# A fused cross-attention and mixture-of-experts kernel: first loads in another order, two elementwise steps on other engines

## The chip, the cores and the metric

The kernel runs on one core of one Trainium2 chip. Its work is shared by TensorE (matrix products and transposes), VectorE, ScalarE and GpSimd (elementwise work and reductions) and the DMA engines; SyncE (SP) only issues transfers. Each engine works through its own queue in order and waits, at the head of that queue, for what the instruction there needs. The metric is the device time of one execution in microseconds (us).

## The reference, cut to what matters

`x` has 4 batches of 512 rows with 512 features; `ctx` has 4 batches of 1601 rows. All is float32.

```python
x = x + xattn(layernorm(x), ctx)          # 16 heads of 32 features
x = x + moe(layernorm(x))                 # 32 experts, 4 per row, and a shared part

def xattn(x, ctx):
    img, txt = ctx[:, :257], ctx[:, 257:]
    q = rms_norm(x @ q_w.T + q_b) * norm_q_w
    k, k_img = rms_norm(...) of txt and img, each with weights of its own
    v, v_img = txt @ v_w.T + v_b, img @ v_img_w.T + v_img_b
    return (softmax(q k / sqrt(32)) v + softmax(q k_img / sqrt(32)) v_img) @ o_w.T + o_b
```

The experts: a router picks 4 of 32 per row, each expert takes at most 80 rows; its two products, SiLU and a third product follow, weighted and added into the output.

## The kernel before, in words

The order of the instructions is written out by hand; each engine's queue follows the order of the calls in the source.

**Opening.** `ones`, `ident_b`, `pick`, `late`, `sums` and `parts` are small constants, filled on VectorE (`ones` on GpSimd) in L140 to L169. Then the loads are issued, all on SP's queue: two tiles of x (`load_x`, 128 rows each), the query weights `q_w`, the columns `q_b` and `norm_q_w` (`column`, L171: 512 numbers laid out as 128 partitions by 4), two more tiles of x, `k_w`, and so on (L195 to L204). A bias column is read with a step, so that it consists of 512 pieces of 4 bytes. VectorE then scales `norm_q_w` (L207) and adds the two value biases (L209, `v_b`).

**Queries.** `queries` (L484) makes for each of a batch's four tiles of x a triple from `turned_x` (L270): *measure* (mean and variance on VectorE, L219 and L221, then 1/sqrt on GpSimd in two instructions, L213 and L214), *norm* (subtract the mean and scale, L227, VectorE) and *turn* (four transposes on TensorE, L285, and a copy on ScalarE, L286). `feature_chunk` (L234) follows: products with the weights (L238), a square with bias on ScalarE (L242) and bias and weight on VectorE (L243). For the first batch the triples run one after another (L503). For each later batch they are done during the attention of the batch before it, in the loop described next.

**Attention.** Per batch, the keys of four blocks of context are made first (`keys`, stages named (block, chunk) in `side`). Then come four groups c = 0 to 3 of four heads each, with 13 tiles t of 128 keys. A step t does on TensorE: the scores from which VectorE takes the row maxima of the *next* group (`wave`, L328, maxima L342 and L344), the weighted sums of tile t-2 (`weighted`, L387), this tile's scores again, shifted by the maxima (L376 and L379), whose exponentials ScalarE takes (L380); and some filling work, the values of the next group (L298) or, at c = 3, the next batch's queries. GpSimd adds up the exponentials (`added`, L395, two instructions of 128x1024 per step); at c = 3 VectorE does that. At the end of a group `split` cuts the maxima in three bfloat16 parts (L349 to L359), which TensorE turns (L365). Matmul results go round eight PSUM banks, less those that hold the running outputs.

`later` is a list of due work: `later.after(n, f)` runs f at the n-th following call of `later.step()`, of which there is one per step t, per key chunk and, after the last batch, per unit of the shared part. `normalize` (L421) uses it: the denominators of a group go through DRAM, VectorE inverts them (L429), SP fetches the result spread over the partitions (`rb`, four transfers, L433), GpSimd multiplies the two outputs (text and image, tiles `po_s` in SBUF) by it (L436, L437), and one step later VectorE adds both and the value bias (L438) into `aoT`, which the output product reads.

At c = 2 the next batch's x is prepared: tile i is loaded at t = 3i, measured at 3i+1, normalized at 3i+2 and turned at 3i+3 (L662 and L671 to L680).

**Rest.** `residual` (L446) projects the attention's output, adds x and the bias `o_b`, takes the second layer norm (with the same `moments` and `centred`) and the router's logits. After the last batch the shared part runs in `units`, with the routing beside it on VectorE, then the 32 experts, whose weights are streamed in.

Of the kernel before, what the change touches and what calls it, by code (L numbers as in the profile page):

```python
# [9 lines left out]
F32 = mybir.dt.float32  # L10
BF16 = mybir.dt.bfloat16
# [7 lines left out]
P = 128  # L19
# [59 lines left out]
        body(tc, a, ident, mhalf, logits, x1_d, xw_d, xnT_d, den_d, rec_d, out)  # L79


class Later:


# [19 lines left out]
def body(ctx, tc, a, ident, mhalf, logits, x1_d, xw_d, xnT_d, den_d, rec_d, out):  # L104
# [31 lines left out]
    def held(name):  # L136
        return hold.tile([P, D], F32, name=name, tag="hold")


    ones = w.tile([P, P], F32, name="ones")  # L140
    nc.gpsimd.memset(ones, 1.0)
    ident_b = w.tile([P, P], BF16, name="ident_b")
    nc.vector.tensor_copy(ident_b, ident)

    pick = w.tile([P, 3, P], BF16, name="pick")
    nc.vector.memset(pick, 0.0)
    for r in range(0, P, HD):
        nc.vector.memset(pick[r:r + 3, 0, :], 1.0)
        nc.vector.memset(pick[r:r + 6, 1:3, :], 1.0)
        nc.vector.memset(pick[r:r + 3, 2, :], 0.0)  # L150
        nc.vector.memset(pick[r:r + 3, 1, HALF:], 0.0)

    late = w.tile([P, HALF], BF16, name="late")
    nc.vector.memset(late, 0.0)
    for r in range(0, P, HD):
        nc.vector.memset(late[r:r + 3, :], 1.0)
        nc.vector.tensor_copy(pick[r:r + 6, 1, :HALF], late[r:r + 6, :])

    sums = w.tile([P, 3, 2, HD // 2], F32, name="sums")
    nc.vector.memset(sums, 0.0)  # L160
    nc.vector.memset(sums[:, 0, 0, :], 1.0)
    nc.vector.memset(sums[:HALF, 1, 0, :], 1.0)
    nc.vector.memset(sums[HALF:, 1, 1, :], 1.0)
    nc.vector.memset(sums[:, 2, 1, :], 1.0)
    parts = []
    for n in range(2):
        t = w.tile([P, NQ, P], BF16, name=f"parts{n}", tag=f"parts{n}")
        nc.vector.memset(t, 0.0)
        parts.append(t)  # L169

    def column(name, src=None):  # L171
        t = w.tile([P, NC], F32, name=name, tag=name)
        nc.sync.dma_start(t, a[name] if src is None else src)
        return t

    def bias_column(name):
        return column(name, a[name].rearrange("(c p) -> p c", p=P))

    def weight(name, tile_=None, tag=None):
        t = w.tile([P, NC, D], F32, name=name, tag=tag or name) if tile_ is None else tile_  # L180
        nc.sync.dma_start(t, a[name])
        return t

    def load_x(b, qt):
        xt = rowt("xt")
        nc.sync.dma_start(xt, a["x"][b, qt * P:(qt + 1) * P, :])
        return xt
# [4 lines left out]
        nc.sync.dma_start(cT, a["ctxT"][b, :, s0:s0 + n].rearrange("(c p) t -> p c t", p=P))  # L192
        return cT

    first_x = [load_x(0, qt) for qt in range(2)]  # L195
    wq = weight("q_w")
    q_b, nq_w = bias_column("q_b"), column("norm_q_w")
    first_x += [load_x(0, qt) for qt in range(2, NQ)]
    first_wk = weight("k_w", wide("wk"))
    k_b, nk_w = bias_column("k_b"), column("norm_k_w")  # L200
    first_block = load_block(0, 0)
    wv = weight("v_w")
    ki_b, nki_w = bias_column("k_img_b"), column("norm_k_img_w")
    v_b, vi_b = bias_column("v_b"), bias_column("v_img_b")  # L204
    o_b = w.tile([P, D], F32, name="o_b")
    rw = w.tile([P, NC, E], F32, name="rw")
    nc.vector.tensor_scalar(nq_w, nq_w, SM_SCALE, None, ALU.mult)  # L207

    nc.vector.tensor_tensor(v_b, v_b, vi_b, ALU.add)  # L209

    def inv_sqrt(r, v, scale, eps):
        n = r.shape[1]
# [3 lines left out]
    def moments(src):  # L216

        stats = st.tile([P, 6], F32, name="stats")
        nc.vector.bn_stats(stats, src)  # L219
        mv = st.tile([P, 2], F32, name="mv")  # L220
        nc.vector.bn_aggr(mv, stats)  # L221
        r = st.tile([P, 1], F32, name="rstd")
        inv_sqrt(r, mv[:, 1:2], 1.0, 1e-5)
        return mv[:, 0:1], r

    def centred(dst, src, moments):
        nc.vector.tensor_scalar(dst, src, *moments, ALU.subtract, ALU.mult)  # L227

    def project(ps, lhsT, rhs):

# [39 lines left out]
    def turned_x(xlT, qt, xt):  # L270

        got = []

        def measure():
            got.append(moments(xt()))

        def norm():
            xl = rowt("xl")
            centred(xl, xt(), got.pop())
            got.append(xl)  # L280

        def turn():
            ps = psum()
            for c in range(NC):
                nc.tensor.transpose(ps[:, c * P:(c + 1) * P], got[0][:, c * P:(c + 1) * P], ident)  # L285
            nc.scalar.copy(xlT[:, :, qt * P:(qt + 1) * P], ps.rearrange("p (c t) -> p c t", c=NC))  # L286

        return measure, norm, turn
# [132 lines left out]
    def normalize(i, c, aoT, po_t, po_i, den):  # L421

        nc.sync.dma_start(den_d[i], den[0:P:HD // 2, :])
        dn = st.tile([P, 2 * NG4 * L // P], F32, name="dn")
        nc.sync.dma_start(dn, den_d[i].rearrange("r (k q) -> (r k) q", k=P // (2 * NG4)))

        def invert():
            rc = st.tile([P, 2 * NG4 * L // P], F32, name="rc")
            nc.vector.reciprocal(rc, dn)  # L429
            nc.sync.dma_start(rec_d[i].rearrange("r (k q) -> (r k) q", k=P // (2 * NG4)), rc)  # L430
            rb = mid.tile([P, 2, L], F32, name="rb")
            for g in range(NG4):
                nc.sync.dma_start(rb[g * HD:(g + 1) * HD], rec_d[i, 2 * g:2 * g + 2, :].partition_broadcast(HD))  # L433

            def scale():
                nc.gpsimd.tensor_tensor(po_t, po_t, rb[:, 0, :], ALU.mult)  # L436
                nc.gpsimd.tensor_tensor(po_i, po_i, rb[:, 1, :], ALU.mult)  # L437
                later.after(1, lambda: nc.vector.scalar_tensor_tensor(  # L438
                    aoT[:, c, :], po_t, v_b[:, c:c + 1], po_i, ALU.add, ALU.add
                ))  # L440

            later.after(2, scale)

        later.after(2, invert)
# [55 lines left out]
        return [partial(value_tile, v, c, t, cTs, ws) for t in range(NKT)]  # L500

    qT, sq_q, turn, work = queries(0, first_x, L)
    for f in [f for parts in turn for f in parts] + work:  # L503
        f()
    pending = []
    for b in range(B):
        kT = kv.tile([P, NC, S], F32, name="kT")
# [4 lines left out]
        rest = [[]] * NQ  # L512
        if b == 0:
            wvi = weight("v_img_w")
            nc.sync.dma_start(o_b, a["o_b"].partition_broadcast(P))
            nc.sync.dma_start(rw, a["router_w"])
        else:
            wo = weight("o_w", wide("wo"))
            rest = [residual(b - 1, qt, aoT, lambda wo=wo: wo) for qt in range(NQ)]
# [81 lines left out]
        for c in range(NC):  # L601
# [30 lines left out]
            for t in range(NKT):  # L632
                pT = wide("pT")
                pTs.append(pT)
                if more:
                    wave(c + 1, t, qT, kT, mx)
                if t == 0 and c:
                    mT = shifts(part, nc.scalar.copy)
                if t in (0, 2) and pending:
                    pending.pop(0)()  # L640
                if t == 1:
                    if more:
                        v_next = kv.tile([P, NKT, P], F32, name="v", bufs=2)
                        fill = values(v_next, c + 1, cTs, ws)
                        fill[0]()
                        done = 1
                    elif b + 1 < B:
                        fill = work
                if t > 1:
                    consume(t - 2)  # L650
                exps(c, t, qT, kT, mT, pT)
                if t == 0 and pending:
                    pending.pop(0)()
                if t == 2:
                    g["acc"] = begun(pTs, not more)
                elif 2 < t <= MIX:
                    added(g["acc"], pTs[t - 1], slice(0, P), not more)
                elif t == NKT - 1 and not more:
                    added(g["acc"], pTs[MIX], slice(0, HALF), True)
                if c == 0 and t < 3:  # L660
                    rest[t]()
                if c == NC - 2 and b + 1 < B and t and t % 3 == 0:  # L662
                    turn[t // 3 - 1][2]()
                while t and done * (NKT - 1) < len(fill) * t:
                    fill[done]()
                    done += 1
                later.step()
                if more and t == NKT - 1:
                    part = parts[(c + 1) % 2]
                    split(mx, part, NM)  # L670
                if c == NC - 2 and b + 1 < B:  # L671
                    if t == 0:
                        xs = []
                        qT_next, sq_next, turn, work = queries(b + 1, xs, P)
                    if t % 3 == 0 and t < 3 * NQ:
                        xs.append(load_x(b + 1, t // 3))
                    if t % 3 == 1 and t < 3 * NQ:
                        turn[t // 3][0]()
                    if t % 3 == 2:
                        turn[t // 3][1]()  # L680

            def image(consume=consume, pTs=pTs, idle=not more):

# [356 lines left out]
```

## Time and profile before

| | |
|---|---|
| time, median of 3 runs | 1780.51 us (1779.47 to 1783.83) |
| profiled execution, its own time | 1803.62 us |
| its span, first to last instruction | 1801.9 us |
| mean granted TensorE clock in it | 0.984 |
| TensorE (PE) busy | 1709.7 us, 95% |
| VectorE (DVE) busy | 1002.6 us, 56% |
| GpSimd (POOL) busy | 830.4 us, 46% |
| ScalarE (ACT) busy | 621.7 us, 35% |
| first TensorE instruction | 22.52 us |

In the timeline a line is: start, duration, engine, line of the source, operation, output<-inputs, sizes, and in brackets how long the engine had been idle and what ended that. A line with "x4" merges four instructions in a row. In the view of waits the three figures are the sum in us, how often, and the longest. In the windows each engine has its busy time and, in brackets, the instructions that began; the last three figures are the granted TensorE clock, the DMA share and GB/s. SPq and the like are an engine's queue issuing a transfer.

### The profile page before, as it was taken

The page shows a single profiled execution, that of the slowest core. Times are in us where ns is not written, and L with a number is a line of the kernel's source. Part 1 is how long each engine was busy: PE and PEld are TensorE (multiplying, and loading weights), DVE is VectorE, ACT ScalarE, POOL GpSimd, SP SyncE. Part 2 cuts the span into 40 slices and gives each one's busy share as a digit, 9 for nine tenths or more (in the row PEclk, how much of TensorE's full clock was granted, in tenths as well). Part 3 has the DMA queues.
Part 4 walks back from the last instruction along what each step waited for, and adds up shares of the span by engine and source line. Part 5 has one row for each costly group of instructions (what it writes and reads, how often), then busy time and mean ns, then how long its engine had stood idle before and what let it go on. Part 6 is the DMA issues. An engine that isn't in the chain of part 4 may idle for free. (4 is left out here: it accounts for less than half of the span.)

```text
span 1801.9 us, 29352 instructions
## 1 busy us (share of the span) xinstructions
PE 1709.7 (95%) x11825; PEld 899.0 (50%) x11825; DVE 1002.6 (56%) x1893; ACT 621.7 (35%) x1336; POOL 830.4 (46%) x564
## 2 busy tenths in 40 slices
PE   4999999999999999999999999998999999999886
PEld 2564444445644444565444445643442454477664
DVE  2485666658556657675566558556556668511110
ACT  1114444631254555114554631254456110011111
POOL 1319759322379662327679422377681100123332
PEclk9999999999999999999999999999999999999998
DMA  6000000040100003120001040300011363389894
GB/s 220 1 1 1 20 1 31 15 156 30 65 1 20 31 2 119 50 77 18 20 1 32 14 156 13 105 1 14 2 59 60 114 207 105 100 263 283 272 287 103
DMA packets 68023, 138.38 MB, mean 77 GB/s; under 512 B 16048, under 2 KB 28464, under 8 KB 65584
## 3 DMA queue, kind: packets, MB, share of 16 engines
q1 hardware_dynamic: 62768, 125.70, 20.7%
q0 software_dynamic: 5120, 10.82, 2.9%
q8 instruction: 93, 1.52, 0.3%
q14 instruction: 42, 0.34, 0.1%
HBM read 113.68 MB, written 22.81 MB: 76 GB/s over the span
## 5 line engine op out<-in xcount | busy, mean ns | idle before, releaser
L380 ACT ACTIVATE pT<-ps 128x512 f32<-128x512 f32 (+1 forms) x832 | 429.7, 603 | 385.7 <-PE ps L379 377.4
L342 DVE TENSOR_REDUCE mx<-ps 128x1 f32<-128x512 f32 (+1 forms) x576 | 330.5, 615 | 255.8 <-PE ps L328 255.8
L395 POOL TENSOR_TENSOR acc<-acc,pT 128x1024 f32<-128x1024 f32 x192 | 449.5, 2377 | 14.4 <-ACT pT L380 13.8
L298 PEld LDWEIGHTS ps<-v_w,cT 128*128 128x128 f32 (+1 forms) x1408 | 170.5, 188 | 103.2 <-DVE mx L342 55.3
L387 PE MATMUL po<-pT,v 128*32 128x512 f32 (+2 forms) x1792 | 221.9, 603 | 0.0
L379 PE MATMUL ps<-qT,kT 32*128 32x512 f32 (+1 forms) x1664 | 218.0, 594 | 0.0
L328 PE MATMUL ps<-kT,qT 32*128 32x512 f32 (+1 forms) x1536 | 205.1, 550 | 0.0
L298 PE MATMUL ps<-v_w,cT 128*128 128x128 f32 (+1 forms) x1408 | 199.0, 286 | 0.0
L238 PE MATMUL ps<-cT,wk 128*128 128x512 f32 (+1 forms) x384 | 153.9, 546 | 0.0
L316 DVE TENSOR_REDUCE mx<-ps 128x1 f32<-128x512 f32 (+2 forms) x256 | 128.2, 564 | 7.3 <-PE ps L313 7.2
L914 POOL DMA_INDIRECT out<-y,tok x32 | 45.4, 1420 | 146.4 <-DMA out<-y,tok 72.3
L376 PE MATMUL ps<-mT,pick 32*128 32x512 bf16 (+1 forms) x832 | 86.7, 386 | 23.0 <-DVE mx L342 19.6
L395 POOL TENSOR_TENSOR pT<-pT 65x1024 f32<-65x1024 f32 x24 | 56.0, 2352 | 109.1 <-PE po L387 89.4
L245 POOL TENSOR_TENSOR sq_k<-sq_k,sq 128x512 f32<-128x512 f32 (+2 forms) x48 | 49.6, 1033 | 122.6 <-ACT sq L242 122.6
L376 PEld LDWEIGHTS <-pick 32*128 32x128 bf16 (+1 forms) x832 | 21.8, 91 | 167.4 <-issue 164.1
L238 PEld LDWEIGHTS ps<-cT,wk 128*128 128x128 f32 x384 | 69.6, 190 | 70.5 <-issue 54.3
L904 DVE TENSOR_TENSOR ehT<-ehT,ps 128x160 f32<-128x160 f32 x32 | 10.3, 321 | 164.1 <-ACT ehT L903 164.1
L306 ACT COPY v<-ps 128x128 f32<-128x128 f32 (+1 forms) x208 | 59.7, 287 | 117.4 <-PE ps L298 116.8
L328 PEld LDWEIGHTS ps<-kT,qT 32*128 32x128 f32 x1536 | 80.4, 184 | 31.1 <-issue 10.4
L379 PEld LDWEIGHTS ps<-qT,kT 32*128 32x128 f32 (+1 forms) x1664 | 81.5, 181 | 27.4 <-issue 23.1
L387 PEld LDWEIGHTS po<-pT,v 128*32 128x32 f32 (+2 forms) x1792 | 34.6, 107 | 119.1 <-issue 109.8
L402 POOL TENSOR_TENSOR acc<-pT 128x1024 f32<-128x1024 f32 x24 | 56.7, 2386 | 79.8 <-ACT pT L380 55.3
(176 smaller groups left out, 2187.6 us busy)
## 6 DMA issues: line engine op xcount, KB each, us to landing
W_gate<-in_W_gate SPq DMA_DIRECT2D x32, 512.0 KB, 5.7
W_up<-in_W_up SPq DMA_DIRECT2D x32, 512.0 KB, 6.7
W_down<-in_W_down SPq DMA_DIRECT2D x32, 512.0 KB, 5.5
xt<-in_x SPq DMA_DIRECT2D x32, 256.0 KB, 2.8
cT<-in_ctxT SPq DMA_DIRECT2D x8, 1024.0 KB, 8.4
rb<-rec_d SPq DMA_DIRECT2D x64, 128.0 KB, 2.7
wk<-in_k_w SPq DMA_DIRECT2D x4, 1024.0 KB
wki<-in_k_img_w SPq DMA_DIRECT2D x4, 1024.0 KB, 10.2
```

Of the source, the lines that this page charges most:

```text
L238: nc.tensor.matmul(ps[:, :n], lhsT=wt[:, k, c * P:(c + 1) * P], rhs=xT[:, k, to], start=k == 0, stop=k == NC - 1)
L298: nc.tensor.matmul(ps[lo:hi, :], lhsT=cTs[bl][:, k, at:at + hi - lo], rhs=ws[bl == NB - 1][:, k, c * P:(c + 1) * P], start=k == 0, stop=k ...
L306: nc.scalar.copy(v[:n, t, :], ps[:n])
L316: nc.vector.tensor_reduce(mx[:, qt, g, bl:bl + 1], ps[:, :n], AX.X, ALU.max, negate=True)
L328: nc.tensor.matmul(ps[:, j * n:(j + 1) * n], lhsT=qT[r:r + HD, c, q * P:(q + 1) * P], rhs=kT[r:r + HD, c, k0:k0 + n], start=True, stop=True,)
L342: nc.vector.tensor_reduce(mx[:, qt, g, i:i + 1], ps[:, :m], AX.X, ALU.max, negate=True)
L376: nc.tensor.matmul(ps[:n], lhsT=pick[r:r + HD, kind(t), :n], rhs=mT[r:r + HD, :], start=True, stop=False)
L379: nc.tensor.matmul(ps[:n], lhsT=kT[r:r + HD, c, t * P:t * P + n], rhs=qT[r:r + HD, c, :], start=False, stop=True)
L380: nc.scalar.activation(pT[:n, g, :], ps[:n], AF.Exp)
L387: nc.tensor.matmul(po[r:r + HD, :], lhsT=v[rows, t, r:r + HD], rhs=pT[rows, g, :], start=start, stop=stop)
L395: (nc.vector if idle else nc.gpsimd).tensor_tensor(to[rows, h, :], to[rows, h, :], pT[rows, h, :], ALU.add)
L402: (nc.vector if idle else nc.gpsimd).tensor_tensor(acc[:, h, :], pTs[0][:, h, :], pTs[1][:, h, :], ALU.add)
```

## The change

- All four tiles of x are loaded first, then `q_w` in four pieces; `k_w`, the context and the other weights follow on SP as before. The columns and `o_b` are issued on ScalarE's queue.
- The constants and the addition of the value biases come after the first batch's query projection, the scaling of `norm_q_w` after its norms. For the first batch all four tiles are measured first.
- `moments` also gives `off` = -mean * rstd (one GpSimd instruction more, for the output's norm too), and the norm of the queries is a ScalarE activation, scale * x + off. `centred` (VectorE) stays for the output's norm.
- In `normalize`, GpSimd adds the two outputs, and two steps after the scaling ScalarE adds the bias.
- At c = 2 the next batch's steps have tables for their places: loads at t = 0, 1, 5, 7, measures at 2, 4, 7, 9, norms at 4, 6, 9, 11, turns at 5, 7, 10, 12.

```diff
+LOAD, MEASURE, NORM, TURN = (0, 1, 5, 7), (2, 4, 7, 9), (4, 6, 9, 11), (5, 7, 10, 12)
...
-    ones = w.tile([P, P], F32, name="ones")
...
     def column(name, src=None):
         t = w.tile([P, NC], F32, name=name, tag=name)
-        nc.sync.dma_start(t, a[name] if src is None else src)
+        nc.scalar.dma_start(t, a[name] if src is None else src)
...
-    first_x = [load_x(0, qt) for qt in range(2)]
-    wq = weight("q_w")
+    first_x = [load_x(0, qt) for qt in range(NQ)]
+    wq = w.tile([P, NC, D], F32, name="q_w")
+    for k in range(NC):
+        nc.sync.dma_start(wq[:, k, :], a["q_w"][:, k, :])
     q_b, nq_w = bias_column("q_b"), column("norm_q_w")
-    first_x += [load_x(0, qt) for qt in range(2, NQ)]
+    k_b, nk_w = bias_column("k_b"), column("norm_k_w")
     first_wk = weight("k_w", wide("wk"))
-    k_b, nk_w = bias_column("k_b"), column("norm_k_w")
     first_block = load_block(0, 0)
     wv = weight("v_w")
     ki_b, nki_w = bias_column("k_img_b"), column("norm_k_img_w")
     v_b, vi_b = bias_column("v_b"), bias_column("v_img_b")
     o_b = w.tile([P, D], F32, name="o_b")
+    nc.scalar.dma_start(o_b, a["o_b"].partition_broadcast(P))
     rw = w.tile([P, NC, E], F32, name="rw")
-    nc.vector.tensor_scalar(nq_w, nq_w, SM_SCALE, None, ALU.mult)
-
-    nc.vector.tensor_tensor(v_b, v_b, vi_b, ALU.add)
+    ones = w.tile([P, P], F32, name="ones")
+    nc.gpsimd.memset(ones, 1.0)
...
         inv_sqrt(r, mv[:, 1:2], 1.0, 1e-5)
-        return mv[:, 0:1], r
+        off = st.tile([P, 1], F32, name="off")
+        nc.gpsimd.tensor_scalar(off, mv[:, 0:1], r, -1.0, ALU.mult, ALU.mult)
+        return mv[:, 0:1], r, off
...
         def norm():
             xl = rowt("xl")
-            centred(xl, xt(), got.pop())
+            _, r, off = got.pop()
+            nc.scalar.activation(xl, xt(), AF.Identity, bias=off, scale=r)
             got.append(xl)
...
                 nc.gpsimd.tensor_tensor(po_i, po_i, rb[:, 1, :], ALU.mult)
-                later.after(1, lambda: nc.vector.scalar_tensor_tensor(
-                    aoT[:, c, :], po_t, v_b[:, c:c + 1], po_i, ALU.add, ALU.add
-                ))
+                nc.gpsimd.tensor_tensor(po_t, po_t, po_i, ALU.add)
+                later.after(2, lambda: nc.scalar.activation(aoT[:, c, :], po_t, AF.Identity, bias=v_b[:, c:c + 1]))
...
     qT, sq_q, turn, work = queries(0, first_x, L)
-    for f in [f for parts in turn for f in parts] + work:
+    for measure, _, _ in turn:
+        measure()
+    for _, norm, turned in turn:
+        norm()
+        turned()
+    nc.vector.tensor_scalar(nq_w, nq_w, SM_SCALE, None, ALU.mult)
+    for f in work:
         f()
+    ident_b = w.tile([P, P], BF16, name="ident_b")
...
+    nc.vector.tensor_tensor(v_b, v_b, vi_b, ALU.add)
...
-                if c == NC - 2 and b + 1 < B and t and t % 3 == 0:
-                    turn[t // 3 - 1][2]()
+                prepares = c == NC - 2 and b + 1 < B
+                if prepares and t in TURN:
+                    turn[TURN.index(t)][2]()
...
-                    if t % 3 == 0 and t < 3 * NQ:
-                        xs.append(load_x(b + 1, t // 3))
-                    if t % 3 == 1 and t < 3 * NQ:
-                        turn[t // 3][0]()
-                    if t % 3 == 2:
-                        turn[t // 3][1]()
+                    if t in LOAD:
+                        xs.append(load_x(b + 1, LOAD.index(t)))
+                    if t in MEASURE:
+                        turn[MEASURE.index(t)][0]()
+                    if t in NORM:
+                        turn[NORM.index(t)][1]()
```

More of the change, by code (lines that the diff above doesn't have):

```diff
@@ L137, in held @@
         return hold.tile([P, D], F32, name=name, tag="hold")
-    ones = w.tile([P, P], F32, name="ones")
[L141 to L169, printed above, removed]
     def column(name, src=None):
         t = w.tile([P, NC], F32, name=name, tag=name)
-        nc.sync.dma_start(t, a[name] if src is None else src)
+        nc.scalar.dma_start(t, a[name] if src is None else src)
         return t
@@ L223, in moments @@
         inv_sqrt(r, mv[:, 1:2], 1.0, 1e-5)
-        return mv[:, 0:1], r
+        off = st.tile([P, 1], F32, name="off")
+        nc.gpsimd.tensor_scalar(off, mv[:, 0:1], r, -1.0, ALU.mult, ALU.mult)
+        return mv[:, 0:1], r, off
     def centred(dst, src, moments):
-        nc.vector.tensor_scalar(dst, src, *moments, ALU.subtract, ALU.mult)
+        nc.vector.tensor_scalar(dst, src, *moments[:2], ALU.subtract, ALU.mult)
     def project(ps, lhsT, rhs):
@@ L502, in body @@
     qT, sq_q, turn, work = queries(0, first_x, L)
-    for f in [f for parts in turn for f in parts] + work:
-        f()
+    for measure, _, _ in turn:
[5 more added lines that the diff above has]
+    for f in work:
+        f()
+    ident_b = w.tile([P, P], BF16, name="ident_b")
+    nc.vector.tensor_copy(ident_b, ident)
+    pick = w.tile([P, 3, P], BF16, name="pick")
+    nc.vector.memset(pick, 0.0)
+    for r in range(0, P, HD):
+        nc.vector.memset(pick[r:r + 3, 0, :], 1.0)
+        nc.vector.memset(pick[r:r + 6, 1:3, :], 1.0)
+        nc.vector.memset(pick[r:r + 3, 2, :], 0.0)
+        nc.vector.memset(pick[r:r + 3, 1, HALF:], 0.0)
+    late = w.tile([P, HALF], BF16, name="late")
+    nc.vector.memset(late, 0.0)
+    for r in range(0, P, HD):
+        nc.vector.memset(late[r:r + 3, :], 1.0)
+        nc.vector.tensor_copy(pick[r:r + 6, 1, :HALF], late[r:r + 6, :])
+    sums = w.tile([P, 3, 2, HD // 2], F32, name="sums")
+    nc.vector.memset(sums, 0.0)
+    nc.vector.memset(sums[:, 0, 0, :], 1.0)
+    nc.vector.memset(sums[:HALF, 1, 0, :], 1.0)
+    nc.vector.memset(sums[HALF:, 1, 1, :], 1.0)
+    nc.vector.memset(sums[:, 2, 1, :], 1.0)
+    parts = []
+    for n in range(2):
+        t = w.tile([P, NQ, P], BF16, name=f"parts{n}", tag=f"parts{n}")
+        nc.vector.memset(t, 0.0)
+        parts.append(t)
+    nc.vector.tensor_tensor(v_b, v_b, vi_b, ALU.add)
     pending = []
@@ L514, in body @@
             wvi = weight("v_img_w")
-            nc.sync.dma_start(o_b, a["o_b"].partition_broadcast(P))
             nc.sync.dma_start(rw, a["router_w"])
@@ L670, in body @@
                     split(mx, part, NM)
-                if c == NC - 2 and b + 1 < B:
+                if prepares:
                     if t == 0:
```

## The prediction

> **What bounds the kernel.** I read the page's busy line first, then the stretches, then who waited for whom on TensorE, then the timeline around each gap.
>
> ```profile
> PE 1709.7 (95%) x11825; PEld 899.0 (50%) x11825; DVE 1002.6 (56%) x1893; ACT 621.7 (35%) x1336; POOL 830.4 (46%) x564
> ```
>
> TensorE is busy for 95% of the span, and in most 40 us stretches for all 40. So an edit pays only where TensorE stands still or runs at the half clock. The view of waits, for TensorE, names what it stands still for:
>
> ```profile
> PE ps L285 <- DVE xl L227: 26.1, 4, 22.5
> PE ps L376 <- DVE mx L342: 19.6, 8, 6.5
> PE ps L232 <- DMA xT<-xnT_d: 3.8, 1, 3.8
> ```
>
> The first row is the opening. Its timeline:
>
> ```profile
> 13.10 2.21 SPq L173 DMA_DIRECT2D v_img_b<-in_v_img_b  x1
> ...
> 19.96 0.16 DVE L209 TENSOR_TENSOR v_b<-v_b,v_img_b 128x4 f32<-128x4 f32 x1 [10.83 <-DMA v_img_b<-in_v_img_b]
> 20.04 0.69 DVE L219 BATCH_NORM_STATS2 stats<-xt 128x6 f32<-128x512 f32 x1
> ...
> 22.52 1.12 PE L285 MATMUL ps<-ident,xl 128*128 128x128 f32 x4 [22.52 <-DVE xl L227]
> ...
> 31.26 15.51 PE L238 MATMUL ps<-xlT,q_w 128*128 128x512 f32 x32 [0.68 <-ACT xlT L286]
> ```
>
> VectorE stands at the addition of two bias columns (L209) until 19.96, because the second column is the sixteenth DMA on SP's queue; the statistics of x sit behind it, though x, issued first, takes 2.8 us to land. Then four tiles go round one by one, each about 2.31 us, and the query matmuls start at 31.26.
>
> The second row is the attention. The timeline of the worst place, all engines:
>
> ```profile
> 218.13 9.27 POOL L395 TENSOR_TENSOR acc<-acc,pT 128x1024 f32<-128x1024 f32 x4
> ...
> 218.51 9.44 DVE L438 SCALAR_TENSOR_TENSOR aoT<-po_s,v_b 128x512 f32<-128x512 f32 x1
> ...
> 228.60 0.58 PE L376 MATMUL ps<-mT,pick 32*128 32x512 bf16 x1 [6.48 <-DVE mx L342]
> 228.60 2.28 PE L379 MATMUL ps<-qT,kT 32*128 32x512 f32 x8
> ```
>
> The sum of the two attention outputs (L438) takes 0.75 us when nothing disturbs it; here it takes 9.44, as long as GpSimd's four additions beside it. The maxima (L342) behind it don't free their banks, and TensorE stops for 6.48 us. The windows show the second price, the clock:
>
> ```profile
> 222.00:226.00 4.00, 0.12 (x3) 0.00 (x0) 4.00 (x1) 0.00 (x0) 4.00 (x3) 0.93 0.00 0
> 226.00:230.00 4.00, 1.40 (x9) 0.71 (x8) 4.00 (x5) 0.00 (x0) 1.40 (x1) 0.50 0.00 0
> 230.00:234.00 4.00, 4.00 (x25) 2.13 (x24) 0.58 (x2) 2.22 (x5) 2.00 (x1) 0.71 0.00 0
> ```
>
> The last figures of a line are clock, DMA share and GB/s. After the stop TensorE runs at half clock until about 232.3: the eight matmuls of L379 take 2.28 us, elsewhere 1.03.
>
> **The change, part by part.**
>
> **1. The opening.** VectorE's block before L209 (1.54 to 7.67, 6.1 us) moves behind the query projection. The columns leave SP: their eight issues stood there for 0.43 + 0.51 + 0.46 + 0.74 + 0.45 + 0.67 + 1.48 + 2.21 = 6.95 us. They go to ScalarE's queue, with o_b (0.65): nine issues now stand ahead of the first normalization, which ScalarE also does. SP issues four x tiles at once (about 0.42 each), so x0 lands near 3.6 and its scale and offset are ready after 0.69 + 0.18 (L219, L221), 0.19 + 0.58 (L213, L214), a new offset at L213's 0.19, and some 0.4 of handovers: about 5.9.
>
> But ScalarE must have issued its nine. SP's waits show one issue held until q_w landed (1.4 us) and one until wk landed (0.4): the 11th DMA waits for the 3rd, the 16th for the 8th, so each seems to wait for the one eight before it. If that count runs over both queues, the 16th DMA of the new order, k_img_b, waits for the 8th, q_w's last quarter. q_w landed at 8.6 (issue 1.70 plus 6.9); half a megabyte more of x ahead of it, at the 299 to 307 GB/s of 2 to 6 us, is 1.7: 10.2. Five issues remain (0.45 + 0.67 + about 0.45 twice + 0.65 = 2.7): 12.9. The table load (1.28, now at 0.79) may fall behind them; I take half: 13.5.
>
> Then four rounds, all on ScalarE and TensorE in turn: normalization 0.69 (nearest row L242 at 128x512 with a bias: 687 ns), transposes 1.12, copy 0.59, handovers 0.05: 2.45 each, 9.8. The query matmuls start at 23.3 in place of 31.3: **8.0 us gained.** Bounds: if ScalarE's queue counts for itself, it is free at about 7, matmuls start at 16.8, gain 14.5; if the last columns stand as long as on SP (1.48 and 2.21) and the whole table load comes after, 17.0 + 9.8, gain 4.5. I stay near the second, since both held issues fit the shared count.
>
> The Trainium skill, "DMA: Bandwidth & Descriptors", section "Issuing engines are not separate DMA queues", speaks against this part: queues of several engines end on the same sixteen DMA engines, and a second one saves only the sequencer's issue time. By the rule the split gives SP 6.95 us that nobody waited for, and costs ScalarE as much: nothing or less. By the rows the gain comes from the order, not the bandwidth: L209's 10.83 us no longer stand ahead of x. The rule is why I take 8 and not 14.
>
> Cover: k_w and the first block were issued at 5.21 and 8.57 and landed by 16.0; keys start 15.5 us after the query matmuls, near 38. The 6.1 us block now precedes the first key features on VectorE; it had 2.6 us idle between such steps, so it runs some 3.5 us late and catches up over two; TensorE has eight banks, 3.4 us each, so nothing shows. Without that cover it would cost up to 3.5.
>
> **2. Sums of both outputs, 16 times.** L438 leaves VectorE. GpSimd gets an addition priced like L437 (1.27), ScalarE an activation (0.69) one step later. What L438 costs TensorE now, from the timeline's gaps: 6.48 twice (222 and 1251), with the half clock after it: 3.7 us at half speed the first time and 5.5 the second, so 1.85 + 2.75; and 1.21 three times (293, 634, 974). Sum 12.96 + 4.6 + 3.63 = **21.2 us.**
>
> Here the skill and the trace differ: "SBUF — State Buffer" says of VectorE and GpSimd's shared ports (section "Who interferes with whom") that whoever starts first has them for its whole instruction and the other fully blocks. By it L438 waits for one addition at most, 2.36 + 0.75 = 3.1 us, as 2.52 and 2.83 elsewhere; the four banks in hand hide all but 1.2, so sixteen would be worth 5 x 1.21 = 6. The two rows of 9.44 lasted four additions. The measurement decides: 21.2. The new addition queues behind GpSimd's own, and by the same section ScalarE waits for nobody's port.
>
> **3. Next queries on ScalarE, 12 times, with other steps.** L227 there took 1.16, 0.97, 2.57 and 0.55 per batch, beside the same additions. TensorE's gaps behind it: 1.02 three times and 0.46 twice, **4.0 us.** ScalarE has about 2.3 us free per step (it waits that long for L379), takes 0.69, and the transposes come a step later.
>
> **4. What comes in.** GpSimd gets 16 x 1.27 + 32 offsets at 0.2 to 0.25 (the sixteen of the output norms too) = 27 us over the whole. Mostly it idles there, but in the third group of heads it runs without a gap from 283 to 316.6, and its last addition ends 3.6 us before VectorE splits the maxima (at 319.3), whose small casts and subtractions also need two SBUF reads. It gets 1.27 + about 1.0 later, TensorE 2.2 earlier: they overlap by about 1 us. I take 1 us back in each of three batches: **-3.** Bounds: 0 to 2.4 (one addition) each. At the end of the last batch VectorE adds without pause and GpSimd has three operations instead of two between: L438's 0.75 and its wait of 2.40 go, three waits of 1.27 come, 3.8: xT is requested 0.7 later: **-0.7**, between +3 and -2. SP's queue is passed by no DMA elsewhere except the x loads, a few steps earlier, with DMA idle there.
>
> Sum: 8.0 + 21.2 + 4.0 - 3.0 - 0.7 = 29.5. Of the profiled execution (1801.9 us span, 1.7 around it, 1803.6) 1774 would be left. The median of the runs is 23 us below that execution. I carry the difference over: 1780.5 - 29.5 = **1751.**
>
> **Rivals.**
> (a) The two long stalls are not in the timed runs. For it: 2 x 8.8 = 17.6 us is most of the 23; batches two and three have the same instructions at the same place with 2.52 and no stop of TensorE, so it hangs on nanoseconds. Against: first and last batch agree to the figure (9.44 and 6.48 twice), and the stretch after 1580, with DMA at 0.85 of its time, can be slowed by a profile too. Then 29.5 - 17.6 = 11.9: **1769.**
> (b) The opening gains all: ScalarE free at 7. **1744.**
> (c) The parts about GpSimd do nothing: its additions stay back to back, the splits now stall in place of L438. Only the opening counts: **1772.**
> (d) Slower: ScalarE's in-order queue. Its new activation waits for GpSimd's addition, and the exponentials of the next step stand behind it. At present GpSimd is done with L437 within some 3 us of its issue in the program's order and the activation comes two steps (9 us) later, so it needs a lag over 6 us more. Decides from 29.5 / 16 = 1.8 us of block per group; at 2.5 it is 1780.5 + 10 = **1790.**
>
> **How the numbers follow.** Forecast (all rows hold in the timed runs) 0.50; (a) 0.25; (b) 0.10; (c) 0.09; (d) 0.06. A difference under 0.3% (5.3 us) can't be told from none by this measurement. Only (d) is not faster, and a mild form of it is the same: faster 0.94, same 0.02, slower 0.04. The forecast with its bounds spans 1742 to 1758; with (a), (b) and most of (c) the range is 1740 to 1772.
>
> **What would show it.** L238's first query matmul near 23 (17: own count; 27: queue full). No L438; no TensorE gap near 222, 293, 1251, and no half clock between the opening and 1380. GpSimd's new addition at 1.27; no exponential with a long wait behind the activation. The split's casts (L357) above 0.2 would show the give-back. Wrong would be: gaps of TensorE with ScalarE's or GpSimd's name in the attention, or unchanged time with the long gaps gone, which is (a).

## The result and the profile after

| | before | after |
|---|---|---|
| median of 4 runs | 1781.45 us (1779.47 to 1783.83) | 1761.19 us (1755.5 to 1762.81) |
| ratio of the times | | 0.9874, 95% interval 0.9855 to 0.9892 |
| a second comparison, same kernels, another chip | 1785.0 us | 1759.63 us, ratio 0.9859 (0.9838 to 0.9879) |
| profiled execution | 1803.62 us, span 1801.9 | 1755.5 us, span 1753.8 |

The change saves 20 to 25 us: 20 by the medians of the first comparison, 22 by its ratio, 25 by the second. The forecast was 1751 with a range of 1740 to 1772, so the time lies in the range, 10 us above the point. The two profiled executions differ by 48 us. That is more than the change is worth: the profiled execution of before was not a typical one (experiment 1), and that of after was the fastest of its four. Below, a gain over the kernel before is worked out from the ratio, a difference between two changed kernels from their medians.

The page's busy line of the changed kernel:

```profile
PE 1699.4 (97%) x11825; PEld 895.0 (51%) x11825; DVE 954.3 (54%) x1861; ACT 642.4 (37%) x1368; POOL 866.2 (49%) x612
```

GpSimd carries 36 us more, VectorE 48 less. TensorE's waits between 40 and 1400 us, the changed kernel:

```profile
PE ps L352 <- ACT pT L356: 2.9, 1, 2.9
PE ps L352 <- ACT mT L343: 2.4, 4, 0.6
PE ps L447 <- DVE xn L202: 1.8, 3, 0.6
```

(L352, L355 and L356 are L376, L379 and L380 of before.) The row "DVE mx", 19.6 us in the profile of before and 6.7 in a typical one (experiment 1), is gone, and so is the wait for xT. New is one wait of 2.9 us for ScalarE. The opening, from the changed kernel's timeline:

```profile
2.87 0.46 ACTq L145 DMA_DIRECT2D k_img_b<-in_k_img_b  x1
4.21 0.35 ACTq L145 DMA_DIRECT2D norm_k_img_w<-in_norm_k_img_w  x1
4.21 0.69 DVE L192 BATCH_NORM_STATS2 stats<-xt 128x6 f32<-128x512 f32 x1 [4.21 <-DMA xt<-in_x]
...
6.85 0.52 ACTq L179 DMA_DIRECT2D o_b<-in_o_b  x1
...
7.40 1.28 ACT L255 ACT_TABLE_LOAD   x1 [7.40 <-DMA norm_k_img_w<-in_norm_k_img_w]
...
8.70 0.81 ACT L255 ACTIVATE xl<-xt,off,rstd 128x512 f32<-128x512 f32 x1
...
9.56 1.12 PE L261 MATMUL ps<-ident,xl 128*128 128x128 f32 x4 [9.56 <-ACT xl L255]
...
10.72 0.58 ACT L262 COPY xlT<-ps 128x512 f32<-128x512 f32 x1 [1.21 <-PE ps L261]
...
18.86 15.73 PE L213 MATMUL ps<-xlT,q_w 128*128 128x512 f32 x32 [0.68 <-ACT xlT L262]
```

ScalarE issues its nine transfers until 7.37, loads its table, and does the first norm at 8.70. After four rounds of norm, transposes and copy, 2.50 us each, the query matmuls start, at 18.86 in place of 31.26.

### The profile page after: what moved, and what is told of

The parts are those of the page before. It is cut to its first block, busy times and chain, and to the rows that moved or that the text cites. A ratio compares the mean times of both kernels' runs of the same rounds, so it can differ in the third digit from the quotient of the medians.

```text
span 1753.8 us, 29354 instructions
## 1 busy us (share of the span) xinstructions
PE 1699.4 (97%) x11825; PEld 895.0 (51%) x11825; DVE 954.3 (54%) x1861; ACT 642.4 (37%) x1368; POOL 866.2 (49%) x612
## 5 line engine op out<-in xcount | busy, mean ns | idle before, releaser
L356 ACT ACTIVATE pT<-ps 128x512 f32<-128x512 f32 (+1 forms) x832 | 429.4, 604 | 344.0 <-PE ps L355 333.6
L355 PE MATMUL ps<-qT,kT 32*128 32x512 f32 (+1 forms) x1664 | 214.0, 587 | 0.0
L352 PEld LDWEIGHTS <-pick 32*128 32x128 bf16 (+1 forms) x832 | 21.6, 91 | 165.7 <-issue 164.0
L371 DVE TENSOR_TENSOR acc<-acc,pT 128x1024 f32<-128x1024 f32 (+1 forms) x72 | 97.8, 1405 | 2.1 <-ACT pT L356 2.1
L915 DVE TENSOR_TENSOR ehT<-ehT,ps 128x160 f32<-128x160 f32 x32 | 10.3, 321 | 162.0 <-ACT ehT L914 162.0
L890 POOL DMA_INDIRECT xp<-xw_d,tok x32 | 30.0, 937 | 120.3 <-DVE tok L835 110.8
```

The costliest lines, as they stand in the source:

```text
L355: nc.tensor.matmul(ps[:n], lhsT=kT[r:r + HD, c, t * P:t * P + n], rhs=qT[r:r + HD, c, :], start=False, stop=True)
L356: nc.scalar.activation(pT[:n, g, :], ps[:n], AF.Exp)
L371: (nc.vector if idle else nc.gpsimd).tensor_tensor(to[rows, h, :], to[rows, h, :], pT[rows, h, :], ALU.add)
```

## The experiments

Every profile can be cut at the same points of the program. This table gives the time from one mark to the next in us: the start of the query matmuls, and three stretches that change. "Third group" is from the first matmul of L376 in c = 2 to that in c = 3, for batches one to three; "tail" is from the last group's first to the first matmul of the shared part.

| kernel | query matmuls at | third groups | tail |
|---|---|---|---|
| before, profile above | 31.26 | 65.5, 66.2, 66.2 | 35.3 |
| again_before | 32.06 | 67.4, 66.3, 66.3 | 35.2 |
| after | 18.86 | 62.8, 62.8, 63.1 | 35.1 |
| changed_again (the same kernel) | 18.83 | 62.8, 62.8, 63.1 | 37.5 |
| open_only | 18.72 | 67.0, 66.8, 65.6 | 34.9 |
| sums_only | 32.34 | 68.1, 69.2, 68.6 | 36.3 |
| norms_only | 31.35 | 64.5, 64.5, 64.5 | 35.0 |
| no_sums | 18.82 | 64.5, 64.5, 64.5 | 35.0 |
| one_input | 31.99 | 67.8, 66.5, 67.0 | 34.4 |
| old_places | 18.70 | 65.0, 65.2, 66.1 | 35.0 |
| columns_sp | 15.90 | 62.8, 62.8, 62.8 | 36.1 |
| late_bias | 18.74 | 62.8, 62.8, 63.1 | 35.0 |
| best | 12.19 | 62.8, 62.8, 62.8 | 35.1 |

The other groups and the key stages agree within 2 us throughout, but for the two stalls of the first profile: the groups that hold them take 70.2 and 70.7 us there, 61.8 and 61.5 in again_before. The tails of after and changed_again, one kernel, differ by 2.4 us; in both TensorE stops for 2.86 us near 1335, and over the 4 us that follow the granted clock is 1.00 in the one and 0.50 in the other. The experts, from their first matmul to TensorE's last, take 200.5 to 208.4 us with no order in it, so that single executions differ by several us there and the medians are to be used.

### 1. The kernel before, once more

> The kernel before, unchanged, to see a typical execution. Theory 1 (the two long stalls of 6.48 us, with the half clock behind them worth 17.6 us together, belong to the one profiled execution of 1803.6 us and not to the others): this execution takes about 1780 to 1784 us, L438 shows no 9.44 us and TensorE no gap near 222 and 1251. Theory 2 (they are in every execution, and the 23 us between profile and runs lie elsewhere): L438 shows 9.44 us twice again, also in an execution near 1781 us.

Measured: median 1783.78 us, ratio to before 0.9999 (0.9988 to 1.001). Two places of its timeline:

```profile
219.41 2.53 DVE L438 SCALAR_TENSOR_TENSOR aoT<-po_s,v_b 128x512 f32<-128x512 f32 x1
...
285.44 2.84 DVE L438 SCALAR_TENSOR_TENSOR aoT<-po_s,v_b 128x512 f32<-128x512 f32 x1 [1.62 <-POOL po_s L437]
...
288.93 0.37 PE L376 MATMUL ps<-mT,pick 32*128 32x512 bf16 x1 [1.20 <-DVE mx L342]
```

The sum that took 9.44 us takes 2.53 at the same place of the program, and TensorE doesn't stop there. What stays are the short gaps of the third groups; TensorE's waits between 40 and 1400 us name them:

```profile
PE ps L376 <- DVE mx L342: 6.7, 6, 1.2
PE ps L376 <- DVE mx L344: 2.7, 3, 1.7
```

Theory 1 holds. The same instruction stands in three kernels below (open_only, norms_only, no_sums): of the 64 in these four profiles the longest takes 2.84 us. None of the other runs of the kernel before, up to 1792.6 us, came near 1803.6. Why the sum waited for four additions of GpSimd in that one execution and elsewhere for one is not settled; no run here brought it about on purpose.

### 2. Each part alone

The opening alone: x first, the columns and o_b on ScalarE's queue, q_w in four pieces, the constants behind the query projection, and the first four tiles measured ahead and normed on ScalarE:

```diff
+    first_x = [load_x(0, qt) for qt in range(NQ)]
...
```

> Only the opening of the change: loads in the new order, columns and o_b on ScalarE's queue, all four tiles measured first and normalized on ScalarE for the first batch, constants after the query projection. Sums and the later batches' norms stay as before. In the profile of the change the query matmuls start at 18.86 us in place of 31.26. If a shift at the start is carried to the end: 12.4 us less, 1769 us. If part of it is given back (loads that TensorE catches up with, the constants on VectorE in its way): less than 9 us.

Measured: 1771.11 us, ratio 0.9931 (0.9912 to 0.9951), so 12.3 us of 1785.2. The start is carried to the end. The constants on VectorE cost nothing: TensorE has no gap between 19 us and the third group. The parts of this opening (order, second queue, constants, norm on ScalarE) stand in one run; only the second queue is taken out alone, in experiment 6.

The sums alone:

```diff
-                later.after(1, lambda: nc.vector.scalar_tensor_tensor(
-                    aoT[:, c, :], po_t, v_b[:, c:c + 1], po_i, ALU.add, ALU.add
-                ))
+                nc.gpsimd.tensor_tensor(po_t, po_t, po_i, ALU.add)
+                later.after(2, lambda: nc.scalar.activation(aoT[:, c, :], po_t, AF.Identity, bias=v_b[:, c:c + 1]))
```

> Only the sums: GpSimd adds the two outputs, ScalarE adds the bias two steps later. Theory 1: the three gaps of 1.21 us go (3.6 us), and the wait of ScalarE for GpSimd's addition in the last batch, seen in the changed kernel (2.86 us of TensorE), comes in, against the 3.81 us and its half clock before the shared part that go: 1775 to 1779 us. Theory 2: the two long stalls go as well, 1757 to 1761 us.

Measured: 1792.4 us, ratio 1.004 (1.0025 to 1.0056): **slower by 7 us**, which neither theory had. Its timeline in the first batch's third group:

```profile
285.21 9.29 POOL L395 TENSOR_TENSOR acc<-acc,pT 128x1024 f32<-128x1024 f32 x4
...
294.59 0.19 POOL L213 TENSOR_SCALAR rstd<-mv 128x1 f32<-128x1 f32 x1
...
295.45 2.55 DVE L227 TENSOR_SCALAR xl<-xt,mv,rstd 128x512 f32<-128x512 f32 x1 [3.44 <-POOL rstd L214]
...
298.65 0.58 PE L376 MATMUL ps<-mT,pick 32*128 32x512 bf16 x1 [3.38 <-DVE mx L342]
```

VectorE had measured that tile by 287.9. The inverse root stands on GpSimd behind four additions, and these behind the new sum, so it comes at 295.4. VectorE's norm waits at the head of its queue for 3.44 us, then takes 2.55, 2.0 more than its 0.55 in the opening, where GpSimd adds nothing. The maxima are late, TensorE stops for 3.38, and over the next 4 us the granted clock is 0.59 (after the 1.2 us gaps of again_before it stays at 1.00). The 1.2 us gap at the sum has gone, a larger one at the norm has come, in each of three batches:

```profile
PE ps L376 <- DVE mx L342: 10.2, 3, 3.4
```

The third groups take 5.9 us more than those of again_before, the tail 1.1: together the 7.

The next queries' norms alone:

```diff
+LOAD, MEASURE, NORM, TURN = (0, 1, 5, 7), (2, 4, 7, 9), (4, 6, 9, 11), (5, 7, 10, 12)
...
+                nc.scalar.activation(xl, xt(), AF.Identity, bias=off, scale=r)
```

> Only the later batches' norms: offset on GpSimd, activation on ScalarE, the new places of loads, measures, norms and turns. First batch and sums as before. By the gaps behind L227 (1.02 three times, 0.46 twice) 4.0 us less: 1777 us. If the gaps beside the sums (1.21 us each) come from the same crowd on GpSimd's and VectorE's ports and grow, 0 to 2 us less.

Measured: 1779.18 us, ratio 0.9964 (0.9953 to 0.9974): 6.4 us. One gap of 1.4 us per batch is left of three, that at the sum:

```profile
PE ps L385 <- DVE mx L351: 4.2, 3, 1.4
```

### 3. The sums undone, and the whole again

> The changed kernel itself, beside the same runs of the kernel before as the next three, for a narrower interval: theory (opening 12.4 to 13.2 us, third groups of three batches 11.3 us together, end of the last batch and start of the shared part about 1.9) 24 to 26 us less than before; the first runs said 20.

Measured: 1759.63 us, ratio 0.9859 (0.9838 to 0.9879): 25.2 us.

> The change with the sums of both outputs back on VectorE (L438's instruction, one step after the scaling); opening and norms as changed. Theory A (the sums are worth something only where the next norms have left VectorE: alone they were 7 us slower because GpSimd's extra addition made VectorE's norm wait 3.4 us): a third group takes 64.5 us in place of the changed kernel's 62.8, three times, so about 5 us more than the changed kernel. Theory B (the sums cost their 7 us here too): 5 to 7 us less than the changed kernel.

Measured: 1764.47 us, ratio 0.9889 (0.9869 to 0.9908): 4.8 us more than the changed kernel beside it, the third groups at 64.5 as expected. The two intervals overlap by a little; the three stretches differ by 1.4 to 1.7 us each, and the gap at the sum is there again:

```profile
PE ps L352 <- DVE mx L318: 4.2, 3, 1.4
```

Theory A holds: the same edit costs 7 us alone and is worth 5 after the norms have left VectorE for their new places, where nothing on VectorE waits for GpSimd's inverse root in those groups.

### 4. Is it the port?

```diff
-                later.after(1, lambda: nc.vector.scalar_tensor_tensor(
-                    aoT[:, c, :], po_t, v_b[:, c:c + 1], po_i, ALU.add, ALU.add
-                ))
+                big = st.tile([P, 1], F32, name="big")
+                later.after(1, lambda: nc.vector.tensor_reduce(big, po_t, AX.X, ALU.max))
+                later.after(2, lambda: nc.scalar.activation(aoT[:, c, :], po_t, AF.Identity, bias=v_b[:, c:c + 1]))
```

> The kernel before, but in place of the sum VectorE takes the maximum of the text output alone (one input in SBUF, the same 128x512, the same place in its queue, the same wait for GpSimd), and ScalarE writes the text output plus bias, so that the image output is left out of the result. GpSimd has no extra addition. Theory port (the sum is long because its two inputs need the port that GpSimd's additions hold): the instruction takes about 0.7 us always, the 1.20 us gap of TensorE near 287, 628 and 968 us goes, the gaps near 276 and 298 stay: 3 to 5 us less than before. Theory crowd (VectorE is simply late there): 2.5 to 2.8 us and the gap stay.

This kernel leaves the image output out. Measured: 1782.44 us, ratio 0.9986 (0.9973 to 0.9999), 2.5 us less where 3 to 5 were expected. The instruction by its line (duration min/median/max in ns), and the timeline of the norm after it:

```profile
L439 DVE TENSOR_REDUCE big<-po_s x16: 667/675/689, 219.1 to 1395.5; 128x1 f32<-128x512 f32 x16
```

```profile
294.44 2.56 DVE L227 TENSOR_SCALAR xl<-xt,mv,rstd 128x512 f32<-128x512 f32 x1 [2.10 <-POOL rstd L214]
```

The maximum takes at most 0.69 us sixteen times, beside the same additions of GpSimd where the sum took up to 2.84. So the length comes from what the instruction is, not from the place. That the second input alone makes it is not shown: the maximum also writes one column in place of 512, and the norm, which reads one tile, takes 2.56 beside the same additions. Nor is the port itself seen in a trace; it is the name for what such instructions wait for.

The sum's 1.2 us gap is gone. Part of that is a shorter wait: the maximum needs only the first of GpSimd's two products and waits 2.4 us for it in all, the sum 10.3. The time hardly moves, because TensorE then runs ahead of GpSimd, and the norm waits 2.10 us for its root where it waited 0.97 in again_before: the gap there grows from 1.0 to 2.05, and in two of three batches the clock falls after it (0.57 and 0.59 over 4 us). The stall went to the next place. In sums_only it is 3.38: there the root stands behind 1.27 us more of GpSimd's work, which is about the difference.

### 5. The places of the steps

```diff
-LOAD, MEASURE, NORM, TURN = (0, 1, 5, 7), (2, 4, 7, 9), (4, 6, 9, 11), (5, 7, 10, 12)
+LOAD, MEASURE, NORM, TURN = (0, 3, 6, 9), (1, 4, 7, 10), (2, 5, 8, 11), (3, 6, 9, 12)
```

> The change with the old places of the next queries' steps (loads at t = 0, 3, 6, 9, measures at 1, 4, 7, 10, norms one step after the measure, turns one step after the norm); the norms stay on ScalarE. Theory places (the activation alone would stand behind GpSimd's late 1/sqrt and hold up the exponentials): ScalarE waits 2 to 4 us for the offset in the middle of each third group, TensorE has a gap there, a third group takes 64 us or more in place of 62.8. Rival (moving the norm off VectorE is all of the gain, ScalarE has the slack): 62.8 us and the same time as the changed kernel.

Measured: 1767.3 us, ratio 0.9913 (0.9891 to 0.9936), 7 to 8 us more than the changed kernel. Who waits, by the view of L255, and TensorE's waits between 40 and 1400 us:

```profile
  POOL off L198: 13.5, 6
```

```profile
PE ps L261 <- ACT xl L255: 5.3, 6, 1.1
...
PE ps L352 <- DVE mx L320: 2.0, 3, 1.4
```

Twice per batch ScalarE stands some 2.2 us for the offset, and the transposes stand behind it. The new places, with two steps between measure and norm, are part of the gain, not only the engine. No run keeps the norms on VectorE at the new places, so what the engine alone is worth is open.

### 6. The second queue

```diff
-        nc.scalar.dma_start(t, a[name] if src is None else src)
+        nc.sync.dma_start(t, a[name] if src is None else src)
...
-    nc.scalar.dma_start(o_b, a["o_b"].partition_broadcast(P))
+    nc.sync.dma_start(o_b, a["o_b"].partition_broadcast(P))
```

> The change with the columns and o_b issued on SP again, in the same order of the program: behind the four tiles of x and q_w. Theory order (the gain of the opening comes from x first and the bias addition out of its way, the second queue only keeps ScalarE from its norms until 8.7 us): ScalarE's first norm at about 6.5 us and query matmuls at 16.5 to 17.5 in place of 18.86, 1.5 to 2 us less than the changed kernel. Theory queue (SP's issue time is what the split saves): q_w or the columns late, query matmuls after 19 us, more than the changed kernel.

Measured: 1754.84 us, ratio 0.9831 (0.9809 to 0.9853), beside the changed kernel's 0.9859: the start is 2.9 us earlier, more than either theory had; the intervals overlap.

```profile
5.74 0.81 ACT L255 ACTIVATE xl<-xt,off,rstd 128x512 f32<-128x512 f32 x1 [0.93 <-POOL off L198]
...
15.90 4.64 PE L213 MATMUL ps<-xlT,q_w 128*128 128x512 f32 x5 [0.68 <-ACT xlT L262]
```

ScalarE has nothing to issue: it loads its table at 3.53 and then waits 0.93 us for the offset. x landed earlier too (statistics at 3.48, in the change at 4.21). That no column shares the DMA engines with it here is the likely reason; no run shows it apart.

### 7. The last batch, and all together

```diff
-                later.after(2, lambda: nc.scalar.activation(aoT[:, c, :], po_t, AF.Identity, bias=v_b[:, c:c + 1]))
+                later.after(4 if i == B * NC - 2 else 2, lambda: nc.scalar.activation(aoT[:, c, :], po_t, AF.Identity, bias=v_b[:, c:c + 1]))
```

> The change, but in the last batch's third group the bias activation comes four steps after the scaling in place of two. Theory (rival d of the prediction came true in this one place, where a step is 2.2 us and not 4.5: ScalarE stands 3.1 us at the head of its queue for GpSimd's addition, and TensorE 2.86 us behind it near 1332): the gap near 1332 goes, and 1 to 3 us of it stay gained, because xT, which the shared part waits for, is bound by VectorE's additions. Rival: the gap before the shared part (3.8 us in the kernel before) comes back in full and nothing is gained.

Measured: 1759.6 us, ratio 0.986 (0.9839 to 0.9882), as the changed kernel. First the changed kernel's timeline, where ScalarE and TensorE stand for GpSimd's addition:

```profile
1331.29 2.12 POOL L414 TENSOR_TENSOR po_s<-po_s 128x512 f32<-128x512 f32 x1
...
1333.45 0.72 ACT L415 ACTIVATE aoT<-po_s,v_b 128x512 f32<-128x512 f32 x1 [3.08 <-POOL po_s L414]
...
1334.71 0.37 PE L352 MATMUL ps<-mT,pick 32*128 32x512 bf16 x1 [2.86 <-ACT pT L356]
```

and then late_bias:

```profile
1345.24 5.37 PE L207 MATMUL ps<-xT,shared_gate 128*128 128x512 f32 x8 [3.35 <-DMA xT<-xnT_d]
```

The wait for ScalarE is gone, and that for xT is back; the rival holds. SP's transfer of xT waits for VectorE's additions (13.7 us in the view of SP's waits), so that TensorE waits either for ScalarE or for xT.

The combination of columns_sp and late_bias, and in the opening each norm one ahead of the transposes of the tile before:

```diff
-    for _, norm, turned in turn:
-        norm()
-        turned()
+    turn[0][1]()
+    for qt in range(NQ):
+        if qt + 1 < NQ:
+            turn[qt + 1][1]()
+        turn[qt][2]()
...
```

> The change with three additions: columns and o_b on SP as in columns_sp (query matmuls at 15.90 there, 18.86 in the change), the first batch's second norm issued ahead of the first tile's turn and so on, so that ScalarE and TensorE overlap (four rounds of 2.50 us fall to about 6.5 us in all), and the last batch's bias activation two steps later as in late_bias. Expected: query matmuls at 12.5 to 13 us unless q_w lands later, 5 to 6 us less than the changed kernel from the opening, 1 to 3 from the end: 1751 to 1754 us where the changed kernel takes 1759.6.

Measured: 1753.46 us, ratio 0.9825 (0.9805 to 0.9846); columns_sp against another set of runs of before had 0.9831.

```profile
12.19 8.27 PE L213 MATMUL ps<-xlT,q_w 128*128 128x512 f32 x14 [0.68 <-ACT xlT L262]
```

The query matmuls start 6.6 us before those of the change, and the median is 6.1 us lower than that of late_bias, run beside it. Nothing came from the end of the last batch (tail 35.1). Its median is the lowest of all; that it beats columns_sp is shown by the start, not by the time.

## Why the prediction was right or wrong

**What bounds the kernel** was right: TensorE, and an edit counts by TensorE's gaps. But the rows were taken from one execution. Its two long gaps, 17.6 us with the clock, made up 60% of the forecast gain. Their price was right (the two groups are 8.4 and 9.2 us longer than in again_before), but they aren't there in a typical run. That the time still lies in the range is in part luck: without the 17.6 us a gain of 11.9 was left, and 20 to 25 came, because other terms were too small or did not have to be paid.

**1, the opening: 8.0 forecast, 12.4 by the two profiles shown, 12.3 by open_only.** The mechanism was right, the time at which ScalarE is free was too late: 7.37, not 12.9, near the 7 of rival (b). That a transfer waits for an earlier one across both queues agrees with the timeline: norm_k_img_w, sixth on ScalarE's queue and ninth over both, stands from 3.33 until the first, x0, has landed at 4.21, and on SP a tile of x stands 2.2 us for q_b. What failed is which one: the two queues issue side by side, so the columns come early in the count, and norm_k_img_w waits for a tile of x, not k_img_b for q_w's last quarter. What the last three columns waited for the views don't name. The table load came in whole (1.28; half was taken, and (b)'s 16.8 left it out), the norm took 0.81 where the nearest row gave 0.69, and a round 2.50 for 2.45. The rule of the Trainium skill, "DMA: Bandwidth & Descriptors", section "Issuing engines are not separate DMA queues", that issuing from another engine adds no bandwidth, was the better guide on the split: columns_sp shows that the second queue is a loss of 2.9 us at the start, and that the gain comes without it, from the order and from what was moved out of the way; these two are not separated.

**2, the sums: 21.2 forecast.** The 17.6 of it for the long stalls is what rival (a) took out. The rest, 3.63, became a gain of 5 beside the norms (no_sums), but a loss of 7 us alone. That the two parts hang together the working did not see: part 4 priced GpSimd's new 1.27 us at the split, not at the inverse roots, for which VectorE's norm waits in order. The change moved that norm away for another reason, which was luck. The rule of the Trainium skill, "SBUF — State Buffer", section "Who interferes with whom", that the other engine is kept out for one instruction, worth 6 us by the working, fits the typical profiles (2.5 to 2.8 us each); the prediction let one execution overrule it, and the measured 9.44 stays the one exception.

**3, the norms: 4.0 forecast, 6.4 alone.** Right, and undersized: with the norms went VectorE's wait for the root, and the gaps behind L344, 0.9 us in the profile of before, are 2.7 in again_before. The old_places run shows that the new places are needed for the gain.

**4, what comes in: -3.0 and -0.7 forecast.** The overlap with the split came as forecast, in the changed kernel's first batch:

```profile
296.08 0.88 DVE L333 CAST parts<-nm 128x32 bf16<-128x32 f32 x1
```

0.88, 0.83 and 0.54 us in the three batches, where 0.20 is usual. (This cast reads one tile, so the "two SBUF reads" given for it were not its reason.) But TensorE had the slack for it: the only gap there, 0.62 us for mT, is in again_before too, so -3.0 was 0. At the end of the last batch ScalarE stood 3.08 us for GpSimd and TensorE 2.86, a sign that the prediction had named as one of being wrong: rival (d)'s mechanism, in the only group whose steps are mostly 2.2 us long. It replaced the wait for xT; the tail is 35.1 against 35.2 in the profile shown, and 37.5 in changed_again, where the clock fell.

**Carrying the profile's sum to the median** was the step that made the point wrong. The 23 us between the two were a sign that the profiled execution was disturbed, and rival (a) said so with 0.25. Its gain of 11.9 was 8 to 13 us too small: the opening and the norms brought 4.3 and 2.4 more than their terms, the sums some 1.4, and the give-backs of 3.0 and 0.7 didn't come or changed their form, 11.8 in all.

## What to carry to other kernels

When the profiled execution is longer than the runs by as much as its rarest stalls, price these apart, and give the forecast without them. In a stretch where an engine has no idle time a short extra instruction costs what it delays behind it: look for the engine that waits in order for a small result (here a root) queued behind the long additions, and move that wait away before adding work. A DMA queue on a computing engine is paid at the head of that engine's own work: here ScalarE's first norm came at 8.70 us with it and at 5.74 without.

## What was not expected of the hardware

A two-input sum of 128x512 on VectorE, beside back-to-back two-input additions of GpSimd, took 2.5 to 2.8 us where 0.75 is its own time; a maximum over a tile of that size took 0.69 at most. The normalization on ScalarE with a scale and a bias per partition took 0.81 us in the opening and 0.86 in the attention for 128x512 from SBUF, against 0.59 for the copy from PSUM. ScalarE's table load came only when its first activation's turn had come, at 7.40 us, after the nine transfers that it issued.

Whether the clock fell after a stop of TensorE went with the stop's length. Of the stops of 0.9 us and more between 40 and 1400 us in the thirteen profiles, none of up to 1.66 us was followed by a lower clock in the next 4 us. Of nine from 2.03 to 2.86 us six were (0.50 to 0.65), and so were all twelve from 3.35 us on (0.50 to 0.63). Why the same 2.86 us cost the clock in changed_again and not in after, no run shows.
